# SSD layer of a four-layer network: B and C projected once with taps on VectorE, mask added to the decay sums, y summed in PSUM

## The chip, the cores and the metric

The kernel runs on one core of a Trainium2 chip. The core has five engines, each with its own queue of instructions in a fixed order: TensorE (PE in the profile, with its weight loads as PEld), VectorE (DVE), ScalarE (ACT), GpSimd (POOL) and SyncE (SP), which here only issues transfers. An instruction that waits holds up everything behind it in its engine's queue. The metric is the device time of one execution in microseconds (us); the time of a kernel is the median of its runs.

## The reference, cut to what matters

The program is four layers on an image batch of 4 x 96 x 64 x 64: a Mamba block, an SSD layer (Mamba 2, scanned in four directions), a second Mamba block, and a ConvNeXt block. Only the SSD layer is changed. Per direction it computes, for a sequence of 4096 tokens with 96 channels:

```python
zxbcdt = xs @ in_proj_w.T
z = zxbcdt[..., :D_INNER]                                  # 192
xBC = zxbcdt[..., D_INNER:D_INNER + CONV_DIM]              # x 192, B 128, C 128
dt = softplus(zxbcdt[..., D_INNER + CONV_DIM:] + dt_bias)  # 3 heads
xBC = silu(conv_b + sum(conv_w[:, i] * xp[:, i:i + l, :] for i in range(4)))
...
dAc = cumsum(dt * A)                                       # within a chunk
diff = dAc[:, :, :, None, :] - dAc[:, :, None, :, :]
seg = exp(where(mask, diff, -inf))
att = einsum('bcsn,bctn->bcst', Cm, Bm)[..., None] * seg * dt
y = einsum('bcsth,bcthp->bcshp', att, xh)                  # within a chunk
y = y + einsum(..., Cm, exp(dAc), prev)                    # from the carried state
y = rmsnorm((y + D * xh) * silu(z)) @ out_proj_w.T
```

xp is xBC padded by three tokens, so the depthwise convolution has four taps. Results do not depend on the chunk length; the kernel uses 128.

## The kernel before, in words

The whole program is one stream of instructions. The class `Ssd` handles the layer. Four images, two orders (row by row, column by column) and two directions (r = 0 forward, r = 1 reverse) give 16 sequences; each sequence is four blocks of 1024 tokens, and each block eight chunks of 128. That makes 64 blocks and 512 chunks. The normalised input of one order stands in SBUF in `xn`, 96 channels by 4096 tokens, with three zero columns at each end and one row of ones below.

`weights_of` prepares weights once. It multiplies the projection weights of x, B and C by each of the four convolution taps, so that projection and convolution become one product with an inner size of 4 x 96 = 384, which `sconv` holds in three pieces of 128 rows. `stack` fills `pk`, the matching right-hand side: four shifted copies of the input, packed into three pieces of 128 rows by six transfers on SP's queue.

`front` does, for a block, everything that does not depend on the scan. For r = 0 it projects z (L1051) and copies it out. Then for B and C (q = 0, 1) and each half of 512 tokens it accumulates three products of `sconv` with `pk` in a PSUM bank (L1069), which ScalarE copies out with the bias (L1074). Then for each chunk it forms x, token by channel, in three products (L1080) and DVE adds the bias (L1085). Then one Silu over x, B and C (L115, between two loads of function tables), for r = 0 one over z, and B is transposed (L1097, copied by L1099). All of these use two PSUM banks with the tag "front".

Per chunk four stages follow. `decay` takes the cumulative sums of the chunk's tokens, broadcast to all partitions by a transfer (`dr`), subtracts the partition's own sum and clamps at zero (L1118, one DVE instruction per head), and takes one Exp over three heads (L110). `weights` forms C times B in PSUM (L1131), multiplies it with the triangular mask on DVE (L1133), multiplies the decays by that on POOL (L1134), and has POOL form x times dt, x times the state weights and x times D in one instruction (L1138). `outputs` multiplies decays with x for three heads (L1163), multiplies C with the carried state (L1168), scales that on DVE (L1172), adds D times x on POOL (L1173), adds the product within the chunk on DVE (L1174), updates the carried state (L1177 on PE, L1182 on POOL, L1183 on DVE), multiplies with z (L1185), and squares on ScalarE (L1186). `scale`, `by_channels` (L1204, L1206) and `finish` (L1217, L1228) normalise, transpose, project and add into the output, a pair of chunks at a time.

`run` interleaves: per chunk it calls `weights` one chunk ahead, `outputs` for the chunk, `finish` three behind, `decay` two ahead, and after each of these four points takes one step of `front` for the next block; steps end at the `yield`s. `preludes` (normalisation, turning, step sizes of the next sequence) advance likewise. This is only the order in which the program is written; a scheduler then sets the order on each engine, and inserts the waits. Tiles of a tag are reused in turn, so an instruction that writes a tile waits for the readers of the one `bufs` before it: two "front" banks, two "y" banks, four `seg`, three `xs`.

Of the kernel before, what the change touches and what calls it, by code (L numbers as in the profile page):

```python
# [18 lines left out]
F32 = mybir.dt.float32  # L19
# [8 lines left out]
P = 128  # L28
T = 512
# [741 lines left out]
)  # L771


class Ssd:


# [5 lines left out]
    def __init__(self, ctx, tc, k, src, dst, w):  # L782
        nc = self.nc = tc.nc
        self.k, self.w, self.dst = k, w, dst
        self.raw, self.res, self.bn, self.src = src
        one = self.one = ctx.enter_context(tc.tile_pool(name="s1", bufs=1))
        self.work = ctx.enter_context(tc.tile_pool(name="swork", bufs=2))
        self.psum = ctx.enter_context(tc.tile_pool(name="sps", bufs=2, space=PSUM))
        self.dram = ctx.enter_context(tc.tile_pool(name="sdram", bufs=2, space=DRAM))

        self.norm = one.tile([C, 1], F32, name="norm")
        nc.sync.dma_start(self.norm, w["norm"])
        self.ones = one.tile([P, P], F32, name="ones")
        nc.vector.memset(self.ones, 1.0)
        self.eps = one.tile([C, 1], F32, name="epsn")
        nc.vector.memset(self.eps, 1.1920929e-07)

        self.tri = one.tile([P, 2, Q], F32, name="tri")
        for r, step in enumerate((1, -1)):
            nc.gpsimd.affine_select(  # L800
                out=self.tri[:, r], in_=self.ones, compare_op=ALU.is_ge, fill=0.0, base=0,
                pattern=[[step, Q]], channel_multiplier=-step,
            )


        self.xn = [one.tile([C + 1, L + 2 * PAD], F32, name=f"xn{o}") for o in range(2)]
        for x in self.xn:
            nc.vector.memset(x[:C, :PAD], 0.0)
            nc.vector.memset(x[:C, PAD + L :], 0.0)
            nc.gpsimd.memset(x[C : C + 1], 1.0)  # L810
        self.prev = self.pk = None
        self.X = one.tile([C, L], F32, name="X")
        self.batch = None
        self.seq = {}
        self.z = {}

    def weights_of(self, w):
# [3 lines left out]
        nc.sync.dma_start(self.inw, w["in"])  # L821

        conv = self.work.tile([P, 3 * BLK], F32, tag="pk", name="conv")
        conv = conv[:C, : 4 * CONV].rearrange("c (k n) -> c k n", k=4)
        nc.sync.dma_start(conv, w["conv_wT"].partition_broadcast(C))
        yield
        xbc = self.inw[:C, DI : DI + CONV]
        nc.vector.tensor_tensor(conv, conv, xbc[:, None].to_broadcast([C, 4, CONV]), ALU.mult)
        self.conv = one.tile([P, 3, CONV], F32, name="sconv")
        for i, r0, r1, tap, c0 in PIECES:  # L830
            nc.sync.dma_start(self.conv[r0:r1, i], conv[c0 : c0 + r1 - r0, tap])
        self.xbias = one.tile([P, DI], F32, name="xbias")
# [2 lines left out]
        nc.sync.dma_start(  # L835
            self.bcbias, w["in"][C, 2 * DI : 2 * DI + 2 * DST].rearrange("(q p) -> p q", q=2)
        )
        self.ad = one.tile([P, 2, NH], F32, name="ad")
        nc.sync.dma_start(self.ad, w["ad"].partition_broadcast(P))
        self.a = one.tile([P, 1, NH], F32, name="a")  # L840
# [138 lines left out]
    def decays(self, r):  # L979
# [12 lines left out]
        ps = self.bank("front")  # L992
        nc.tensor.matmul(ps[:, :n], lhsT=self.tri[:, r], rhs=da, start=True, stop=True)
        nc.vector.tensor_copy(dac, ps[:, :n])
        nc.tensor.matmul(ps[:, n : 2 * n], lhsT=self.ones, rhs=da, start=True, stop=True)
        k.act.exp_ln(dec, ps[:, n : 2 * n], AF.Exp)
        k.act.exp_ln(edac, dac, AF.Exp)
# [10 lines left out]
        nc.vector.tensor_copy(row, pt)  # L1008
        rows = self.dram.tile([n, Q], F32, name="rows")
        nc.sync.dma_start(rows, row)  # L1010
        return dict(dac=dac, dec=dec, edac=edac, coef=coef, rows=rows)

    def prelude(self, b, o, r):

# [20 lines left out]
    def front(self, b, o, r, blk, made, following):  # L1035
# [26 lines left out]
        pre = self.work.tile([P, n1 + n2], F32, name="pre")  # L1062
        x = made["x"] = pre[:, :n1].rearrange("p (c n) -> p c n", c=QB)
        bc = made["bc"] = pre[:, n1:].rearrange("p (q t) -> p q t", q=2)
        for q in range(2):
            for c in range(BLK // T):
                p = self.bank("front")
                for i in range(3):
                    nc.tensor.matmul(  # L1069
                        p, lhsT=self.conv[:, i, DI + q * DST : DI + (q + 1) * DST],  # L1070
                        rhs=pk[:, i, ds(c * T, T)], start=(i == 0), stop=(i == 2),
                    )
                    yield
                nc.scalar.activation(  # L1074
                    bc[:, q, ds(c * T, T)], p, AF.Identity, bias=self.bcbias[:, q : q + 1]
                )
        for c in range(QB):
            p = self.bank("front")[:, :DI]
            for i in range(3):
# [31 lines left out]
    def decay(self, g):  # L1111

        nc, k = self.nc, self.k
        blk, c, made = g["blk"], g["c"], g["made"]
        n0 = (blk * QB + c) * NH
        seg = g["seg"] = self.work.tile([P, NH, Q], F32, name="seg", bufs=4)
        for h in range(NH):
            nc.vector.tensor_scalar(  # L1118
                seg[:, h], g["pair"]["dr"][:, c % 2 * NH + h],
                made["dac"][:, n0 + h : n0 + h + 1], 0.0, ALU.subtract, ALU.min,  # L1120
            )
        k.act.exp_ln(seg, seg, AF.Exp)

    def weights(self, g):

        nc = self.nc
        c, made, seg = g["c"], g["made"], g["seg"]
        bm, cm = (made["bc"][:, q, ds(c * Q, Q)] for q in range(2))
        self.halves = self.bank("halves").rearrange("p (i n) -> p i n", i=2)
        ps = self.halves[:, 0, :Q]  # L1130
        nc.tensor.matmul(ps, lhsT=bm, rhs=cm, start=True, stop=True)  # L1131
        cb = self.work.tile([P, 1, Q], F32, name="cb")
        nc.vector.tensor_tensor(cb[:, 0], self.tri[:, g["r"]], ps, ALU.mult)  # L1133
        nc.gpsimd.tensor_tensor(seg, seg, cb.to_broadcast([P, NH, Q]), ALU.mult)  # L1134
        xs = self.work.tile([P, 3, NH, HD], F32, name="xs", bufs=3)
        x = made["x"][:, c].rearrange("p (k h d) -> p k h d", k=1, h=NH)
        coef = made["coef"][:, g["blk"] * QB + c, :, :, None]
        nc.gpsimd.tensor_tensor(  # L1138
            xs, x.to_broadcast([P, 3, NH, HD]), coef.to_broadcast([P, 3, NH, HD]), ALU.mult
        )  # L1140
        g["xs"] = xs.rearrange("p k h d -> p k (h d)")

    def outputs(self, g):
# [19 lines left out]
            nc.tensor.matmul(py[:, ch], lhsT=seg[:, h], rhs=xs[:, 0, ch], start=True, stop=True)  # L1163
        y = self.work.tile([P, DI], F32, name="y")
        if first:
            nc.vector.tensor_tensor(y, py[:, :DI], xs[:, 2], ALU.add)
        else:
            nc.tensor.matmul(  # L1168
                py[:, DI : 2 * DI], lhsT=made["bc"][:, 1, ds(c * Q, Q)], rhs=self.prev,
                start=True, stop=True,  # L1170
            )
            nc.vector.tensor_tensor(heads(y), heads(py[:, DI : 2 * DI]), by_head("edac"), ALU.mult)  # L1172
            nc.gpsimd.tensor_tensor(y, y, xs[:, 2], ALU.add)  # L1173
            nc.vector.tensor_tensor(y, y, py[:, :DI], ALU.add)  # L1174
        if not last:
            st = self.halves[:, 1, :DI]
            nc.tensor.matmul(st, lhsT=made["bt"][:, c], rhs=xs[:, 1], start=True, stop=True)  # L1177
# [4 lines left out]
                nc.gpsimd.tensor_tensor(heads(prev), heads(self.prev), by_head("dec"), ALU.mult)  # L1182
                nc.vector.tensor_tensor(prev, prev, st, ALU.add)  # L1183
            self.prev = prev
        nc.vector.tensor_tensor(yz[:, i], y, made["z"][:, c], ALU.mult)  # L1185
        nc.scalar.activation(y, yz[:, i], AF.Square, accum_out=ssq[:, i : i + 1])  # L1186

    def scale(self, g):
# [482 lines left out]
```

## Time and profile before

| | |
|---|---|
| median of 3 runs | 9310.08 us (9306.05 to 9322.33) |
| profiled execution, its own time | 9324.82 us |
| its span, first to last instruction | 9323.1 us |
| mean granted clock of TensorE | 0.925 |
| PE busy | 7912.3 us |
| DVE busy | 7734.4 us |
| POOL busy | 6984.1 us |
| ACT busy | 5461.1 us |
| SSD stage, from its first B/C matmul to about its end | 2864.7 to 5880 us of the span |

The profile comes from one execution. Busy time is the time in which an engine has an instruction running; matmuls overlap, and their ends are modelled, so a sum of matmul durations can exceed the time they took. In a row of groups stand the line, the engine, the operation, output and inputs, shapes and count, then busy time in us and the mean duration of one in ns, then the idle time of the engine just before, and what ended it. A row of a timeline has the start, the time, the engine, the line and the operation.

### The profile page before, as it was taken

The numbers are of one execution on the slowest core, as the hardware profiler recorded it, in microseconds if no ns is written. First come the engines' busy times: TensorE is split into PE (matmuls) and PEld (weight loads), VectorE is DVE, ScalarE is ACT, GpSimd is POOL, SyncE is SP. The second block draws the span as 40 slices with busy tenths as digits, with TensorE's granted clock in tenths as the row PEclk, the third lists the DMA queues.
The fourth block names the chain that finished last, engine by engine and source line by source line (L and its number), as shares of the span: only waits on it lengthen the run. The fifth ranks groups of instructions, "written<-read, shape, count | busy, mean of one in ns | idle before, by whom it ended". The sixth has DMA issues, their size and how long they took to land. (4 is left out here: it accounts for less than half of the span.)

```text
span 9323.1 us, 114005 instructions
## 1 busy us (share of the span) xinstructions
PE 7912.3 (85%) x34968; PEld 3427.8 (37%) x34968; DVE 7734.4 (83%) x9136; ACT 5461.1 (59%) x9510; POOL 6984.1 (75%) x4637
## 2 busy tenths in 40 slices
PE   7888888888878988998898989788888888888588
PEld 1222222222215676676776767412222222222122
DVE  6999999999995676666666667699999999999787
ACT  5667666666654454555545544566766666666255
POOL 6999999999994555555555555599999999999411
PEclk8999999999988998999999999899999999998789
DMA  7888888888873223222322222488888988888643
GB/s 184 217 228 229 220 225 230 221 227 221 224 197 100 68 76 87 69 69 82 86 62 79 82 69 70 113 211 225 230 218 225 234 220 221 231 222 223 153 115 83
DMA packets 799372, 1525.85 MB, mean 164 GB/s; under 512 B 114510, under 2 KB 120042, under 8 KB 795691
## 3 DMA queue, kind: packets, MB, share of 16 engines
q1 hardware_dynamic: 795690, 1513.45, 62.6%
q8 instruction: 280, 4.59, 0.2%
q10 hardware_dynamic: 3072, 5.11, 0.2%
q14 instruction: 330, 2.70, 0.1%
HBM read 1222.94 MB, written 148.50 MB: 147 GB/s over the span
## 5 line engine op out<-in xcount | busy, mean ns | idle before, releaser
L419 POOL TENSOR_TENSOR hc<-hs,bc 128x1024 f32<-128x1024 f32 x1536 | 3606.0, 2364 | 298.1 <-DVE hs L412 287.7
L412 DVE TENSOR_TENSOR_SCAN hs<-da,carry,bs 128x1024 f32<-128x1024 f32 x864 | 2027.4, 2347 | 129.7 <-issue 51.2
L384 PE MATMUL bs<-du,seldu 64*128 64x512 f32 x4608 | 1480.4, 709 | 687.8 <-DVE hs L412 672.0
L407 DVE TENSOR_TENSOR bs<-bs,bc 128x1024 f32<-128x1024 f32 x1152 | 1397.3, 1213 | 19.4 <-PE bs L384 18.5
L110 ACT ACTIVATE da<-da,w_a 128x1024 f32<-128x1024 f32 x1152 | 1301.6, 1138 | 1.5
L384 PEld LDWEIGHTS bs<-du,seldu 64*128 64x128 f32 x4608 | 408.8, 202 | 1766.6 <-issue 887.1
L433 PE MATMUL py<-hc,selsum 128*32 128x512 f32 x6144 | 868.1, 627 | 94.4 <-DVE y L450 70.7
L392 POOL TENSOR_TENSOR du<-du,bc 128x1024 f32<-128x1024 f32 x384 | 909.0, 2367 | 12.6 <-DMA du<-dg 12.6
L1118 DVE TENSOR_SCALAR seg<-dr,dac 128x128 f32<-128x128 f32 x1536 | 639.0, 449 | 296.1 <-PE y L1163 292.5
L1134 POOL TENSOR_TENSOR seg<-seg,cb 128x384 f32<-128x384 f32 x512 | 515.9, 1009 | 475.4 <-DVE cb L1133 409.4
L207 PE MATMUL pu<-h,w_conv 96*64 96x512 f32 (+1 forms) x3072 | 809.4, 646 | 7.8 <-ACT h L196 7.2
L1069 PE MATMUL front<-pk,sconv 128*128 128x512 f32 x1536 | 760.6, 612 | 24.5 <-ACT z L1057 21.0
L110 ACT ACTIVATE bs<-da,w_a 128x1024 f32<-128x1024 f32 x384 | 428.4, 1116 | 585.3 <-DVE hs L412 472.6
L1173 POOL TENSOR_TENSOR y<-y,xs 128x192 f32<-128x192 f32 x496 | 294.6, 594 | 611.7 <-DVE y L1172 594.6
L412 DVE TENSOR_TENSOR_SCAN hs<-bs,carry,du 128x1024 f32<-128x1024 f32 x288 | 670.8, 2329 | 58.9 <-DMA dd<-delta 30.8
L1186 ACT ACTIVATE y<-yz 128x192 f32<-128x192 f32 x512 | 186.1, 363 | 906.7 <-DVE yz L1185 905.7
L412 DVE TENSOR_TENSOR_SCAN hs<-da,bs 128x1024 f32<-128x1024 f32 x288 | 658.6, 2287 | 42.5 <-issue 14.6
L1138 POOL TENSOR_TENSOR xs<-pre,coef 128x576 f32<-128x576 f32 x512 | 598.8, 1174 | 58.1 <-ACT pre L115 25.5
L1080 PE MATMUL front<-sconv,pk 128*128 128x192 f32 x3072 | 572.7, 330 | 54.4 <-DVE pre L1085 49.1
L1080 PEld LDWEIGHTS front<-sconv,pk 128*128 128x128 f32 x3072 | 497.2, 190 | 86.6 <-DVE pre L1085 75.7
L1163 PEld LDWEIGHTS y<-xs,seg 128*128 128x128 f32 x3072 | 440.4, 205 | 144.4 <-issue 83.9
L1163 PE MATMUL y<-xs,seg 128*128 128x64 f32 x3072 | 445.1, 281 | 27.8 <-POOL seg L1134 22.3
(228 smaller groups left out, 13854.6 us busy)
## 6 DMA issues: line engine op xcount, KB each, us to landing
da<-dd SPq DMA_DIRECT2D x3072, 256.0 KB
du<-dg SPq DMA_DIRECT2D x768, 256.0 KB
dr<-rows SPq DMA_DIRECT2D x256, 384.0 KB
bc<-rows SPq DMA_DIRECT2D x256, 256.0 KB
dd<-delta SPq DMA_DIRECT2D x192, 256.0 KB
dg<-du SPq DMA_DIRECT2D x192, 256.0 KB
pk<-xn SPq DMA_DIRECT2D x128, 384.0 KB
pk<-xn SPq DMA_DIRECT2D x128, 256.0 KB
```

The source lines that it names most:

```text
L110: self.last = self.scalar.activation(out, in_, func, **kw)
L207: nc.tensor.matmul(pu[HALFP * i : HALFP * (i + 1)], lhsT=wt["conv"][:kk, tap, D0[j] : D0[j] + HALFP], rhs=h[:kk, ds(i * T + tap, T)], star ...
L384: nc.tensor.matmul(g["bs"][:, i], lhsT=self.sel["du"][rows, g["half"], g["q"]], rhs=g["made"]["du"][rows, g["j"]], start=True, stop=True,)
L392: self.tc.nc.gpsimd.tensor_tensor(g["du"], g["du"], self.b_or_c(g, 0), ALU.mult)
L407: nc.vector.tensor_tensor(dbx, dbx, self.b_or_c(g, 0), ALU.mult)
L412: nc.vector.tensor_tensor_scan(out, da, dbx, init, ALU.mult, ALU.add)
L419: nc.gpsimd.tensor_tensor(g["hc"], hs, self.b_or_c(g, 1), ALU.mult)
L433: nc.tensor.matmul(py[ds(HALFP * i + QUART * x["half"], QUART)], lhsT=self.sel["sum"][:, q], rhs=x["hc"][:, i], start=(q == 0), stop=(q == ...
L1069: nc.tensor.matmul(p, lhsT=self.conv[:, i, DI + q * DST : DI + (q + 1) * DST], rhs=pk[:, i, ds(c * T, T)], start=(i == 0), stop=(i == 2),)
L1080: nc.tensor.matmul(p, lhsT=pk[:, i, ds(c * Q, Q)], rhs=self.conv[:, i, :DI], start=(i == 0), stop=(i == 2),)
L1118: nc.vector.tensor_scalar(seg[:, h], g["pair"]["dr"][:, c % 2 * NH + h], made["dac"][:, n0 + h : n0 + h + 1], 0.0, ALU.subtract, ALU.min,)
L1163: nc.tensor.matmul(py[:, ch], lhsT=seg[:, h], rhs=xs[:, 0, ch], start=True, stop=True)
```

## The change

B and C are no longer convolved by the product. `project` multiplies the plain projection weights with 345 (or 343) columns of `xn`, three more than the 342 (or 340) tokens of a stretch, in one product per stretch; `STRETCHES` cuts the 1024 tokens into three. ScalarE copies the bank out, multiplied by the last tap and with the bias; `convolve` then adds the other three taps, each a multiply-add on DVE that reads the same bank at a shifted column and updates the output in place. `convolve` runs one stretch behind `project`, and so both banks are held in between. The steps (`yield`) of the part are twelve, as before. `sconv` and its preparation shrink to x, and two small loads bring the taps.

In `decay`, POOL adds a mask (0 or -1e30) to the broadcast sums of three heads in one instruction, and ScalarE takes one Exp per head with the negated own sum as its bias (`ndac`). In `weights`, DVE multiplies the decays with the product in PSUM directly; the DVE product with the mask and POOL's product are gone. In `outputs`, y is summed in its PSUM bank, and the product with z reads it from there.

```diff
+STRETCHES = ((0, 342), (342, 342), (684, 340))
@@ __init__
+        self.mask = one.tile([P, 2, 1, Q], F32, name="mask")
+        nc.vector.tensor_scalar(
+            self.mask[:, :, 0], self.tri, 1.0, 1e30, ALU.subtract, ALU.mult
+        )
@@ weights_of
-        conv = conv[:C, : 4 * CONV].rearrange("c (k n) -> c k n", k=4)
-        nc.sync.dma_start(conv, w["conv_wT"].partition_broadcast(C))
+        conv = conv[:C, : 4 * DI].rearrange("c (k n) -> c k n", k=4)
+        nc.sync.dma_start(conv, w["conv_wT"][:, :DI].partition_broadcast(C))
         yield
-        xbc = self.inw[:C, DI : DI + CONV]
-        nc.vector.tensor_tensor(conv, conv, xbc[:, None].to_broadcast([C, 4, CONV]), ALU.mult)
-        self.conv = one.tile([P, 3, CONV], F32, name="sconv")
+        xs = self.inw[:C, DI : 2 * DI]
+        nc.vector.tensor_tensor(conv, conv, xs[:, None].to_broadcast([C, 4, DI]), ALU.mult)
+        self.conv = one.tile([P, 3, DI], F32, name="sconv")
...
+        self.taps = one.tile([P, 2, 4], F32, name="taps")
+        for q in range(2):
+            of = w["conv_wT"][:, DI + q * DST : DI + (q + 1) * DST]
+            nc.sync.dma_start(self.taps[:, q], of.rearrange("k p -> p k"))
@@ decays
+        ndac = self.work.tile([P, n], F32, name="ndac")
+        nc.vector.tensor_scalar_mul(ndac, dac, -1.0)
@@ front
+        begun = []
+
+        def project(q, t0, n):
+            p = self.bank("front")
+            nc.tensor.matmul(
+                p[:, : n + 3], lhsT=self.inw[:C, 2 * DI + q * DST : 2 * DI + (q + 1) * DST],
+                rhs=xn[:C, ds(base + t0 + (0 if r == 0 else PAD), n + 3)], start=True, stop=True,
+            )
+            out = bc[:, q, ds(t0, n)]
+            shifts = [p[:, ds(tap if r == 0 else 3 - tap, n)] for tap in range(4)]
+            nc.scalar.activation(
+                out, shifts[3], AF.Identity, bias=self.bcbias[:, q : q + 1],
+                scale=self.taps[:, q, 3:4],
+            )
+            begun.append((q, out, shifts))
+
+        def convolve():
+            q, out, shifts = begun.pop(0)
+            for tap in range(3):
+                nc.vector.scalar_tensor_tensor(
+                    out, shifts[tap], self.taps[:, q, tap : tap + 1], out, ALU.mult, ALU.add
+                )
+
         for q in range(2):
-            for c in range(BLK // T):
-                p = self.bank("front")
-                for i in range(3):
-                    nc.tensor.matmul(
-                        p, lhsT=self.conv[:, i, DI + q * DST : DI + (q + 1) * DST],
-                        rhs=pk[:, i, ds(c * T, T)], start=(i == 0), stop=(i == 2),
-                    )
+            for t0, n in STRETCHES:
+                project(q, t0, n)
+                yield
+                if len(begun) == 2:
+                    convolve()
                     yield
-                nc.scalar.activation(
-                    bc[:, q, ds(c * T, T)], p, AF.Identity, bias=self.bcbias[:, q : q + 1]
-                )
+        convolve()
+        yield
@@ decay
+        nc.gpsimd.tensor_tensor(
+            seg, g["pair"]["dr"][:, ds(c % 2 * NH, NH)],
+            self.mask[:, g["r"]].to_broadcast([P, NH, Q]), ALU.add,
+        )
         for h in range(NH):
-            nc.vector.tensor_scalar(
-                seg[:, h], g["pair"]["dr"][:, c % 2 * NH + h],
-                made["dac"][:, n0 + h : n0 + h + 1], 0.0, ALU.subtract, ALU.min,
-            )
-        k.act.exp_ln(seg, seg, AF.Exp)
+            k.act.exp_ln(seg[:, h], seg[:, h], AF.Exp, bias=made["ndac"][:, n0 + h : n0 + h + 1])
@@ weights
-        cb = self.work.tile([P, 1, Q], F32, name="cb")
-        nc.vector.tensor_tensor(cb[:, 0], self.tri[:, g["r"]], ps, ALU.mult)
-        nc.gpsimd.tensor_tensor(seg, seg, cb.to_broadcast([P, NH, Q]), ALU.mult)
+        nc.vector.tensor_tensor(seg, seg, ps[:, None].to_broadcast([P, NH, Q]), ALU.mult)
@@ outputs
-            nc.vector.tensor_tensor(y, py[:, :DI], xs[:, 2], ALU.add)
+            nc.vector.tensor_tensor(py[:, :DI], py[:, :DI], xs[:, 2], ALU.add)
...
-            nc.vector.tensor_tensor(y, y, py[:, :DI], ALU.add)
+            nc.vector.tensor_tensor(py[:, :DI], y, py[:, :DI], ALU.add)
...
-        nc.vector.tensor_tensor(yz[:, i], y, made["z"][:, c], ALU.mult)
+        nc.vector.tensor_tensor(yz[:, i], py[:, :DI], made["z"][:, c], ALU.mult)
```

More of the change, by code (lines that the diff above doesn't have):

```diff
@@ L1010, in decays @@
         nc.sync.dma_start(rows, row)
-        return dict(dac=dac, dec=dec, edac=edac, coef=coef, rows=rows)
+        return dict(ndac=ndac, dec=dec, edac=edac, coef=coef, rows=rows)
     def prelude(self, b, o, r):
```

## The prediction

> **What bounds the kernel now.** I read the page first (busy shares, then the 40 slices), then the stretch of time in which the changed code runs, cut into the parts of one block, then the costliest groups on each engine there, and last the timeline of single instructions. The chain that ended last says nothing here: its steps sum to some 6% of the span, at the end, in another stage.
>
> ```profile
> PE 7912.3 (85%) x34968; PEld 3427.8 (37%) x34968; DVE 7734.4 (83%) x9136; ACT 5461.1 (59%) x9510; POOL 6984.1 (75%) x4637
> ...
> PE   7888888888878988998898989788888888888588
> PEld 1222222222215676676776767412222222222122
> DVE  6999999999995676666666667699999999999787
> ...
> POOL 6999999999994555555555555599999999999411
> ```
>
> PEld marks the stage: slices 13 to 25, where weight loads are dense, are the SSD layer. There PE is the fullest engine and DVE and POOL have room. Everywhere else DVE and POOL are at 9, and the change touches nothing there.
>
> ```profile
> 2864.70:5880.00 3015.30, 2707.98 (x14596) 2104.46 (x14594) 2050.36 (x5203) 1523.69 (x3472) 1656.68 (x2008) 0.95 0.26 75
> ...
> 4446.20:4463.00 16.80, 16.75 (x76) 10.91 (x77) 11.99 (x30) 8.38 (x23) 10.00 (x13) 1.00 0.70 202
> 4463.00:4475.10 12.10, 11.47 (x77) 11.16 (x76) 8.41 (x24) 1.81 (x6) 5.09 (x7) 1.00 0.42 107
> 4475.10:4491.40 16.30, 12.40 (x87) 10.80 (x85) 11.60 (x31) 13.79 (x27) 11.87 (x14) 1.00 0.43 125
> ```
>
> Busy times by stretch, in the order PE, weight loads, DVE, ACT, POOL. The first row is the whole SSD stage, 3015 us for 64 blocks, 47.1 us each. The other three are one forward block, cut at its first B/C matmul (L1069), its first x matmul (L1080) and the end of its last: a "BC" stretch of 16.8 us, an "x" stretch of 12.1 and a rest of 16.3, in sum 45.2. In BC, PE has no gap at all; in the rest PE idles, and ACT (13.8 of 16.3, the big Silu and its table loads) is the fullest. A reverse block, cut likewise at 4575.6, is 17.8, 13.5 and 9.1, in sum 40.4. So the stage has two bounds in turn.
>
> ```profile
> L1118 DVE TENSOR_SCALAR seg<-dr,dac 128x128 f32<-128x128 f32 x1519 | 629.0, 447 | 294.9 <-PE y L1163 291.2 <-DMA dr<-rows 3.5
> L1185 DVE TENSOR_TENSOR yz<-y,z 128x192 f32<-128x192 f32 x503 | 421.4, 838 | 9.1
> L1085 DVE TENSOR_TENSOR pre<-front,xbias 128x192 f32<-128x192 f32 x512 | 175.3, 351 | 188.3 <-PE front L1080 188.0
> ...
> L1133 DVE TENSOR_TENSOR cb<-tri,halves 128x128 f32<-128x128 f32 x504 | 140.1, 282 | 190.8 <-PE halves L1131 110.5 <-POOL seg L1134 79.4
> ...
> L1134 POOL TENSOR_TENSOR seg<-seg,cb 128x384 f32<-128x384 f32 x503 | 506.9, 1009 | 472.2 <-DVE cb L1133 408.4 <-ACT seg L110 39.9 <-ACT dtrow L961 8.5
> ...
> 4404.41 1.16 POOL L1138 TENSOR_TENSOR xs<-pre,coef 128x576 f32<-128x576 f32 x1
> ...
> 4404.75 1.02 DVE L1185 TENSOR_TENSOR yz<-y,z 128x192 f32<-128x192 f32 x1
> ```
>
> Groups of the stage, then two timeline rows. L1185 and L1085 have the same size, but L1185, which reads two SBUF tensors, takes 838 ns and L1085, which reads PSUM, 351. The timeline shows why: yz starts while POOL's xs runs and ends 0.2 us after it.
>
> **What the Trainium skill says.** "SBUF — State Buffer", section "SBUF: two separate sides": a DVE instruction with two SBUF inputs and a GpSimd one that reads SBUF lock each other out for a whole instruction. The L1185 rows agree. "VectorE: DVE Perf Modes", "The TRN2 errata": an fp32 tensor_tensor takes (N+151)/0.96 ns; L1085 (192: 357, trace 351) agrees, L1185 does not, being locked. "Perfetto Trace Analysis", "Identifying the Most-Contended Engine": matmul busy time is no good measure of the PE's limit. So I take spacings for PE: weight loads of L1069 begin 0.43 us apart in the timeline, though one matmul is 612 ns on the page.
>
> **The change, part by part, summed over the stage.** PE: each product is two recorded matmuls. Gone are 1536 x 0.43 = 660 us; new are 64 blocks x 6 products x 2 x 0.43 x 345/512 = 223. PE: -437. ACT: three Exp of 128 columns for one of 384. The rows L110 at 1024 (1138 ns) and 384 (518) give 0.97 ns a column, so 128 is 270, +0.29 x 512 = +150 in durations (about 100 in spacing, ACT instructions overlap by 0.1 us in the timeline). L1074 becomes 384 of (675 - 165) = 0.51 instead of 256 of 0.675: +23. POOL: the product by cb becomes the mask's addition in the same shape: 0; bounds from L1182 (192 columns, 574) to L1138 (576, 1174), I take 1009. DVE: L1118 goes, -1536 x 0.447 = -687; cb, -512 x 0.282 = -144; yz, now from PSUM, 0.838 to 0.35, -250. New: the product seg by PSUM, 384 columns, 351 + 192 x 0.984 = 0.54 (slope from L266, 512 columns, 666 ns), +276; 1152 tap instructions of 342 columns from PSUM, 0.50 each, +576. That slope is of a three-operand instruction from PSUM, but none of this size is shown; bounds 0.36 (342 columns at 0.96 a ns and 0.04 of start) and 0.57 (L1463, two SBUF operands, 846 at 512 columns, scaled); I take 0.50. DVE: -229. The in-place sum in PSUM costs what L1174 costs now. At the start two small tap loads go onto SP's queue ahead of the first pk loads (0.41 us each by the bcbias row, and pk is wanted later now); the weight product L828 shrinks from 2.02 to about 0.9 us; ndac is 16 x 0.2 = 3 us. All these run under the normalisation of the first batch, about 30 us; without that cover they'd be 2 to 5 us.
>
> **What of this is on the path.** No engine is full after it, so I follow the order of instructions in the changed program for the same two blocks. The BC work is moved from PE, where it stood back to back, to DVE, and the scheduler now puts 4 chunks of eight into that stretch instead of 2.5.
>
> BC, forward: DVE issues 18 taps x 0.50 = 9.0, four chunks x (4 x 0.35 + 0.54) = 7.8, two copies yt and two additions to X 1.9: 18.7, less 0.04 for each of 40 overlaps (starts are that much closer than durations) 17.1. PE needs only 12 x 0.29 = 3.5 and, for four chunks, 4 x 2.15 = 8.6 (starts in the timeline from 4402.03: y, carried state and new state 1.32 a chunk; L1131 0.22; transposes and output projection 1.2 a pair). What is late next: POOL's mask additions are queued two at a time ahead of y+D*x (L1203), and the second waits for its seg buffer, that is for y matmuls of the next chunk. DVE's sum of y stands behind it, about 1.2 us once a block. Together 18.3, against 16.8.
>
> x: 24 products at 0.325 (12 recorded matmuls start within 1.95) = 7.8, one chunk's matmuls 1.3, a wait for DVE 0.7: 9.8, against 12.1, because fewer chunks are left there.
>
> Rest: ACT from the last x: table 1.28, Silu 3.19, z 1.47, table 1.28, then copies, six or seven Exp at 0.17 spacing, two scalings, 7.6: 14.9, against 16.3. Sum 43.0 against 45.2, -2.2. The reverse block the same way: 21.0, 10.1, 7.3: 38.4 against 40.4, -2.0.
>
> Three blocks of eight carry the next sequence's normalisation or step sizes and are paced by that too; I count half there: 40 x 2.1 + 24 x 1.05 = -109 us, +3 for ndac. Against the profiled span, 9323 - 106 = 9217. That execution took 9324.8, the median is 9310.1, so 9202; I say 9200.
>
> **Rivals.**
> PE is the bound throughout. For: 90% busy, no gap in BC. Against: PE idles in the rest, ACT is full there. Then most of 437 is kept: 8870 to 9050.
>
> Nothing changes: taps on DVE cost each BC stretch what x and rest give. With taps at 0.57 instead of 0.50 a block loses 18 x 0.07 = 1.3 us of the 1.7 that it gains on average. For: DVE sums to 17 us in an 18 us stretch. Against: L266's slope. Time 9285 to 9330.
>
> Slower, by POOL's queue: mask additions now stand ahead of L1203 and wait for matmuls of a later chunk, which wait for DVE, which waits for L1203's result. I have priced one such wait of 1.2. If three of the four rounds of a BC stretch each lose a mask addition and a y addition (1.0 + 0.59), that is 4.8 - 1.2 = 3.6 more than priced, 1.9 net a block, 64 x 1.9 = +122, about 9430. It decides from 1.7 us a block on. For: POOL's L1173 already waits 592 us for DVE in this stage. Against: these waits cost nothing today.
>
> **How the numbers follow.** My case, 9120 to 9290: 0.46. PE's relief mostly kept, under 9120: 0.19. No change: 0.12. Slower, 9330 to 9450: 0.23 (the POOL mechanism at half its price to its full). A measurement of this kernel tells about 0.2% from no change. The likeliest case's own range is 9120 to 9290; leaving out about a tenth at each end of all cases gives 9010 to 9380. Faster 0.65, same 0.12, slower 0.23.
>
> **What would show it.** Right: tap instructions near 0.50 us; yz at 0.35; PE idle in BC, with DVE over 90% busy there; the BC stretch a little longer, x and rest shorter; ACT idle before Silu. Wrong: DVE waiting more than about 1.7 us a block on POOL for y; taps above 0.57; or PE still without a gap in BC, which would mean the bigger gain.

## The result, and the profile after

The changed kernel takes 9185.08 us (median of 4 runs, 9178.76 to 9191.85) against 9308.06 us (median of 4 runs of the kernel before, 9302.81 to 9322.33): a ratio of 0.9866 [0.9849, 0.9883], 123 us less. The prediction was 9200 us. Its own sum was made against the profiled execution of before (9324.82 us); the profiled execution of the changed kernel took 9178.76, 146 less where the sum had 106 less. That pair flatters the change, as the profiled run of before is slower than all four of its timed runs and that of the changed kernel the fastest of its four.

The page of the changed kernel: busy time, share and count of each engine, then two rows of the 40 slices.

```profile
PE 7611.2 (83%) x34200; PEld 3366.9 (37%) x34200; DVE 7597.2 (83%) x8769; ACT 5724.8 (62%) x10662; POOL 6929.5 (76%) x4637
...
PE   7888888888877888888888888788888888888588
DVE  6999999999995666666666667699999999999787
```

PE lost 301 us of busy time, not the 437 of the prediction, which counted spacings; DVE lost 137, ACT gained 264. In the SSD stage (slices 13 to 25) PE no longer reaches 9. From the first to the last block's first B/C matmul the stage went from 2975.0 to 2829.9 us in the timelines, 145 of the 146 us, so everything outside it kept its length.

Busy times by stretch of the changed kernel (columns: PE, weight loads, DVE, ACT, POOL, granted clock, DMA share, GB/s). First most of the stage, then a forward and a reverse block, each as BC, x and rest. The reverse block is the one that the prediction cut, number 37 of the 64. The forward one is number 35, the one after the block that it cut (number 34).

```profile
2867.00:5740.00 2873.00, 2436.42 (x13831) 2052.45 (x13830) 1920.81 (x4852) 1786.21 (x4616) 1605.20 (x2012) 0.91 0.27 79
...
4423.90:4441.50 17.60, 14.33 (x85) 10.92 (x84) 14.26 (x36) 11.97 (x38) 10.95 (x15) 1.00 0.15 46
4441.50:4451.50 10.00, 9.92 (x62) 9.62 (x63) 6.82 (x20) 1.89 (x5) 4.23 (x6) 1.00 0.12 39
4451.50:4468.50 17.00, 13.94 (x82) 12.88 (x81) 7.49 (x20) 13.88 (x31) 9.87 (x12) 0.80 0.42 117
4503.60:4524.40 20.80, 15.88 (x93) 12.21 (x93) 15.62 (x39) 14.88 (x47) 12.24 (x17) 1.00 0.17 55
4524.40:4534.80 10.40, 10.08 (x61) 9.42 (x62) 7.26 (x21) 3.49 (x9) 5.29 (x7) 1.00 0.01 2
4534.80:4540.80 6.00, 5.40 (x44) 4.87 (x42) 3.83 (x11) 5.45 (x6) 4.69 (x6) 1.00 0.64 185
```

PE, which had no gap in BC before, now idles there (14.33 of 17.60). The stretches against the prediction, in us:

| | BC | x | rest | sum |
|---|---|---|---|---|
| forward block, before | 16.8 | 12.1 | 16.3 | 45.2 |
| predicted | 18.3 | 9.8 | 14.9 | 43.0 |
| measured, the block after it | 17.6 | 10.0 | 17.0 | 44.6 |
| that block, before | 16.8 | 12.1 | 17.8 | 46.6 |
| reverse block, before | 17.8 | 13.5 | 9.1 | 40.4 |
| predicted | 21.0 | 10.1 | 7.3 | 38.4 |
| measured | 20.8 | 10.4 | 6.0 | 37.2 |
| mean of all 64 blocks, before | 18.2 | 12.6 | 16.5 | 47.2 |
| mean of all 64 blocks, after | 20.4 | 10.5 | 14.0 | 44.9 |

Block 34 itself took 19.8, 10.0 and 16.1 us in the changed kernel, at a granted clock of 0.74 in its BC, where it had 1.00 before. So I compare block 35 with itself: its rest had a clock of 0.81 before and of 0.80 after. The means of the rest are over 63 blocks, as none follows the last.

The groups of the changed kernel in the stage: on DVE the taps, the product by C times B, and yz; on POOL the mask's addition; on ACT the Exp of one head and the copy with the last tap.

```profile
L1096 DVE SCALAR_TENSOR_TENSOR pre<-front,taps,pre 128x342 f32<-128x342 f32 (+1 forms) x1152 | 619.3, 563 | 49.1 <-ACT pre L1087 38.2 <-DMA gn<-in_L_gnorm 10.5
L1164 DVE TENSOR_TENSOR seg<-seg,halves 128x384 f32<-128x384 f32 x504 | 274.0, 544 | 49.2 <-ACT seg L110 44.4 <-PE halves L1163 4.2
L1215 DVE TENSOR_TENSOR yz<-y,z 128x192 f32<-128x192 f32 x503 | 176.0, 350 | 4.6
L1149 POOL TENSOR_TENSOR seg<-dr,mask 128x384 f32<-128x384 f32 x507 | 507.6, 1001 | 532.8 <-PE y L1193 436.5 <-DVE pre L1096 29.0 <-ACT pre L1087 13.8
L110 ACT ACTIVATE seg<-seg,ndac 128x128 f32<-128x128 f32 x1514 | 516.7, 391 | 51.1 <-POOL seg L1149 50.6
L1087 ACT ACTIVATE pre<-front,bcbias,taps 128x342 f32<-128x342 f32 (+1 forms) x384 | 240.8, 630 | 195.9 <-PE front L1081 192.6 <-DMA rows<-row 1.3
```

Three of the six prices are as predicted: L1164 544 ns (540), yz 350 (350), the mask's addition 1001 (1009). A tap takes 563 where 500 was taken, just within its bound of 570. The two on ACT are off: 391 where 270 was taken, 630 where 510 was.

### The profile page after: what moved, and what is told of

The parts are those of the page before. It is cut to its first block, busy times and chain, and to the rows that moved or that the text cites. A ratio compares the mean times of both kernels' runs of the same rounds, so it can differ in the third digit from the quotient of the medians.

```text
span 9177.0 us, 113399 instructions
## 1 busy us (share of the span) xinstructions
PE 7611.2 (83%) x34200; PEld 3366.9 (37%) x34200; DVE 7597.2 (83%) x8769; ACT 5724.8 (62%) x10662; POOL 6929.5 (76%) x4637
## 5 line engine op out<-in xcount | busy, mean ns | idle before, releaser
L1149 POOL TENSOR_TENSOR seg<-dr,mask 128x384 f32<-128x384 f32 x512 | 512.6, 1001 | 532.8 <-PE y L1193 436.5
L1096 DVE SCALAR_TENSOR_TENSOR pre<-front,taps,pre 128x342 f32<-128x342 f32 (+1 forms) x1152 | 619.3, 563 | 49.1 <-ACT pre L1087 38.2
L110 ACT ACTIVATE seg<-seg,ndac 128x128 f32<-128x128 f32 x1536 | 524.4, 391 | 55.8 <-POOL seg L1149 55.1
L1112 PEld LDWEIGHTS front<-sconv,pk 128*128 128x128 f32 x3072 | 525.0, 198 | 65.3 <-DVE pre L1117 19.2
L1203 POOL TENSOR_TENSOR y<-y,xs 128x192 f32<-128x192 f32 x496 | 294.6, 594 | 290.5 <-DVE y L1202 284.1
L1493 DVE SCALAR_TENSOR_TENSOR acc<-strips,kern,acc 128x512 f32<-128x512 f32 x504 | 424.1, 843 | 53.2 <-ACT acc L1483 36.7
```

The lines of the kernel that those rows point to most:

```text
L110: self.last = self.scalar.activation(out, in_, func, **kw)
L1096: nc.vector.scalar_tensor_tensor(out, shifts[tap], self.taps[:, q, tap : tap + 1], out, ALU.mult, ALU.add)
L1112: nc.tensor.matmul(p, lhsT=pk[:, i, ds(c * Q, Q)], rhs=self.conv[:, i, :DI], start=(i == 0), stop=(i == 2),)
L1493: nc.vector.scalar_tensor_tensor(acc, stacks[i][1][:, y : y + strip, x : x + WW], kern[:, g, tap : tap + 1], acc, ALU.mult, ALU.add,)
```

## The experiments

The change has three parts that can be made alone: B and C by taps ("bc"), the mask addition ("mask"), and y in PSUM ("y"). The first five runs, with the kernels before and after and a seventh, make all eight combinations. Medians are in us; ratios are to the runs of the kernel before that belong to each (their medians lie between 9308.06 and 9314.74), with 95% intervals. "Less" is always against those, and two experiments are compared by what each is less. The intervals are some 15 to 25 us to each side for most of them, so a difference of under 30 us between two is not clear of the noise; where I lean on one, I say what the timelines add.

**y in PSUM alone.** Three operands of the kernel before; the third, in the first chunk of a sequence, goes likewise:

```diff
-            nc.vector.tensor_tensor(y, y, py[:, :DI], ALU.add)
+            nc.vector.tensor_tensor(py[:, :DI], y, py[:, :DI], ALU.add)
-        nc.vector.tensor_tensor(yz[:, i], y, made["z"][:, c], ALU.mult)
+        nc.vector.tensor_tensor(yz[:, i], py[:, :DI], made["z"][:, c], ALU.mult)
```

> The kernel before, with only y summed in its PSUM bank. Theory (two bounds in turn: PE in the BC stretch, ScalarE after the Silu): yz falls from 838 to about 350 ns, DVE loses some 250 us of busy time, and the time hardly moves, 0 to 40 us faster than before, since PE has no gap in BC. Rival (the lock between DVE and POOL holds up the stage): at least 100 us faster. Also: POOL's xs and prev get shorter if they too waited for the lock.

Measured: 9162.65, ratio 0.9842 [0.9821, 0.9863], 146 us less. This part alone gains at least as much as the whole change. The theory of the expectation, by which the product with z was hidden, falls. The groups before, on DVE and POOL (2864 to 5680 us):

```profile
L1185 DVE TENSOR_TENSOR yz<-y,z 128x192 f32<-128x192 f32 x465 | 391.0, 841 | 8.3
...
L1182 POOL TENSOR_TENSOR prev<-prev,dec 128x192 f32<-128x192 f32 x437 | 250.7, 574 | 192.0 <-PE y L1168 161.9 <-DVE seg L1118 13.0 <-DVE prev L1183 11.4
```

and with y in PSUM:

```profile
L1185 DVE TENSOR_TENSOR yz<-y,z 128x192 f32<-128x192 f32 x496 | 174.8, 352 | 9.0
...
L1182 POOL TENSOR_TENSOR prev<-prev,dec 128x192 f32<-128x192 f32 x466 | 239.3, 513 | 122.0 <-PE y L1168 83.7 <-DVE seg L1118 24.4 <-DVE prev L1183 10.7
```

The same instruction takes 352 ns instead of 841, and POOL's update of the state, unchanged in the program, 513 instead of 574. Both sides of a lock became shorter, as the Trainium skill has it ("SBUF — State Buffer", "SBUF: two separate sides": a two-SBUF-input DVE instruction and a GpSimd one that reads SBUF keep each other out).

**The mask addition alone**, from `decay` and `weights` of the change; two small tiles ("da" and "wt") have one buffer instead of two, to make room, here and in the next experiment:

```diff
-            nc.vector.tensor_scalar(seg[:, h], dr[...], dac[...], 0.0, ALU.subtract, ALU.min)
-        k.act.exp_ln(seg, seg, AF.Exp)
+        nc.gpsimd.tensor_tensor(seg, dr[...], self.mask[...], ALU.add)
+        for h in range(NH):
+            k.act.exp_ln(seg[:, h], seg[:, h], AF.Exp, bias=made["ndac"][...])
-        nc.gpsimd.tensor_tensor(seg, seg, cb.to_broadcast([P, NH, Q]), ALU.mult)
+        nc.vector.tensor_tensor(seg, seg, ps[:, None].to_broadcast([P, NH, Q]), ALU.mult)
```

> The kernel before, with only the mask addition on POOL, one Exp per head and the product with PSUM on DVE. Theory: DVE loses some 550 us, ScalarE gains about 340 (Exp of 128 columns 391 ns in the changed kernel), PE keeps its work, so the BC stretch stays PE-bound at 16 to 18 us and the time is within 40 us of before. Rival (DVE is what limits): 100 us faster or more. The rival of POOL's queue: slower than before by over 50 us.

Measured: 9233.81, ratio 0.9915 [0.9897, 0.9932], 75 us less. On average a forward block grew from 44.6 to 46.1 us, all of it in the rest (17.0 to 18.6), where ACT is the fullest engine and now has three Exp for one; a reverse block shrank from 49.9 to 45.4, in its rest too (16.0 to 11.6).

**Both of these**, B and C left on PE:

> The changed kernel without the B and C part. Theory: DVE is down to about 1400 us in the stage and still the time is within 60 us of before, as PE stays without a gap in BC. Rival (these two parts make the whole gain): about 9185.

Measured: 9166.74, ratio 0.9839 [0.982, 0.9857], 142 us less: no faster than y alone. The rows of the stage of this kernel, and then of y alone, in the columns as above:

```profile
2864.00:5720.00 2856.00, 2648.42 (x14532) 2097.85 (x14532) 1432.31 (x3681) 1728.98 (x4470) 1601.38 (x2002) 0.95 0.28 79
```

```profile
2864.00:5740.00 2876.00, 2642.33 (x14711) 2076.40 (x14709) 1841.60 (x5254) 1526.16 (x3508) 1641.18 (x2034) 0.97 0.28 79
```

DVE has 409 us less to do than with y alone, and the time stays; PE is at 93%. This doesn't show that room on DVE is worth nothing with y in PSUM, for the part also gives ACT 203 us more and puts POOL's instruction ahead of the Exp, and it has two effects that cancel: against y alone, forward blocks are 2.1 us longer and reverse ones 1.7 shorter. The same holds in all five pairs of kernels here that differ in the mask addition (in the first two pairs in the two small tiles too): with it the mean forward block is longer, by 1.4 to 2.7 us, and the mean reverse block shorter, by 0.7 to 4.4. The addition in the reverse direction alone was not run.

**B and C by taps alone**, the `front` and `weights_of` parts of the change:

> The kernel before, with only the B and C part. Theory: PE loses its 437 us, but DVE keeps L1118 and the locked yz and gets 1152 taps of 0.56 us, so DVE with some 2600 us of 2900 becomes the bound of the stage: 0 to 200 us slower than before. Rival (PE's relief is the whole gain and DVE has room): 9185 or less.

Measured: 9296.46, ratio 0.9985 [0.9978, 0.9992], 12 us less. The row of its stage:

```profile
2864.00:5720.00 2856.00, 2370.72 (x13231) 1961.25 (x13231) 2280.44 (x6069) 1529.63 (x3460) 1570.61 (x1917) 0.92 0.28 77
```

PE is relieved (83% of the stretch) and DVE is at 80%, with yz, 621 ns here, still a slow one among its work. The mean block has a BC stretch longer by 1.7 us, an x and a rest shorter by 0.9 and 1.3.

**Taps and y, no mask addition:**

> The kernel before with the B and C part and y in PSUM, without the mask addition. The gain of y in PSUM alone was 146 us, of the B and C part alone 12. Theory A (the locked yz was what held the stage, and once it is gone PE's work counts again): the relief of PE now pays, under 9120. Theory B (the BC stretch passes from PE to DVE and gives nothing either way): 9150 to 9180. Theory C (DVE is full with taps and L1118): over 9200.

Measured: 9185.28, ratio 0.986 [0.9845, 0.9875], 129 us less; without its mask addition the changed kernel takes neither more nor less time (6 us between them).

**The changed kernel with y in SBUF as before:**

```diff
-            nc.vector.tensor_tensor(py[:, :DI], y, py[:, :DI], ALU.add)
+            nc.vector.tensor_tensor(y, y, py[:, :DI], ALU.add)
-        nc.vector.tensor_tensor(yz[:, i], py[:, :DI], made["z"][:, c], ALU.mult)
+        nc.vector.tensor_tensor(yz[:, i], y, made["z"][:, c], ALU.mult)
```

> The changed kernel with y summed in SBUF again, so that yz reads two SBUF tensors. If the lock costs what it cost before wherever DVE is the pacing engine: yz back to about 0.8 us, 64 x 8 x 0.45 = 230 us of DVE, and 70 to 200 us slower than the changed kernel (9255 to 9385), that is about level with the kernel before. If the mask addition or the taps carry the gain: under 9230.

Measured: 9273.41, ratio 0.9962 [0.9952, 0.9972], 36 us less; 87 of the 123 are gone with these operands. Its product with z:

```profile
L1215 DVE TENSOR_TENSOR yz<-y,z 128x192 f32<-128x192 f32 x472 | 323.6, 686 | 4.6
```

Here, too, the time follows yz: 686 ns instead of 350. The eight combinations, us against the kernel before:

| | without y | with y |
|---|---|---|
| neither | 0 | -146 |
| mask | -75 | -142 |
| bc | -12 | -129 |
| bc and mask | -36 | -123 |

Reading across, y is worth 67 to 146 us in every row. Reading down the right column, the mask addition adds nothing to it (+4, +6), and moving B and C costs 17 to 19 us (+17, +19), which is about what these runs can tell apart. In the left column that move costs 39 on top of the mask and brings 12 by itself.

The timelines show where the 17 to 19 stand. Eight blocks make the two directions of one image and order, and in the eighth the step sizes and decays of the next sequence are prepared, which need the two "front" banks as well. On top of y, with the mask addition or without it, the move makes an eighth block 8.5 to 8.7 us longer, some 60 us over the seven that have a sequence after them, and saves 0.7 to 1.0 us in each of the 56 others, 40 to 56 us. So in seven blocks of eight the whole move pays, a little; that the banks are the reason in the eighth is read from the timelines and was not tested.

**The changed kernel without its taps.** The three multiply-adds are left out, so B and C are not convolved:

```diff
-            q, out, shifts = begun.pop(0)
-            for tap in range(3):
-                nc.vector.scalar_tensor_tensor(...)
+            begun.pop(0)
```

> The changed kernel with the three tap instructions on DVE left out, so that B and C are not convolved. It prices the taps on the path: 1152 of them at 0.49 us spacing are 564 us of DVE. If the BC stretch is DVE-bound, it falls from 20.4 us to PE's or ScalarE's time, about 13 to 15: 64 x 6 = 380 us faster than the changed kernel, about 8800. If something else paces the stretch (POOL's queue, ScalarE), it is under 150 us faster.

Measured: 8840.49, ratio 0.9492 [0.9476, 0.9508], 474 us less, 351 below the changed kernel. The mean BC stretch falls from 20.4 to 13.2 us, though PE has the same matmuls: the taps set its length in the changed kernel, by DVE's time or by the banks that they keep; this run takes both away.

**Half of it: B as three products on PE, C by taps, y in PSUM, no mask addition.** If the whole move overfills DVE and no move leaves PE full, a part of it should beat both. `sconv` keeps B's columns besides x's.

```diff
+        for c in range(BLK // T):
+            ...            # B, bc[:, 0]: three products on PE, as before
+        for t0, n in STRETCHES:
+            project(1, t0, n)    # C: one product and taps, as in the change
+            ...
```

> As the run before it, but only C is projected with taps; B stays three products on PE. PE loses some 218 us of work, DVE gets 576 taps, about 280 us in spacing. Theory A and B: between y alone (9163) and both; if PE and DVE share the BC stretch evenly, faster than either, 9080 to 9150. Theory C: 9160 to 9200.

Measured: 9067.34, ratio 0.9735 [0.972, 0.975]. That is 247 us less than before, and 124 below the changed kernel: it beats both, and y alone by 101. The row of most of its stage:

```profile
2870.00:5350.00 2480.00, 2221.78 (x12779) 1810.94 (x12778) 1829.62 (x5194) 1385.88 (x3202) 1454.18 (x1807) 0.96 0.29 84
```

PE is at 90% and DVE at 74%. BC takes 18.1 us, x 10.3, the rest 14.6: the shorter x and most of the shorter rest of the change, without the longer BC. Against y alone an eighth block is 3.8 us longer, not 8.7, and the others are 2.2 shorter, not 0.7. So the half gains in both places: there is less on DVE, and the banks are held for less of the stretch. No run parts the two.

**The same half with the mask addition**, that is, the changed kernel with B on PE:

> The changed kernel with B left to three products on PE and only C projected with taps; mask addition and y in PSUM as in the change. If the BC stretch of the changed kernel is paced by DVE (18 taps, of which 9 go) and PE has room for 12 more matmuls of 0.43 us, it shortens by some 2 us a block: 9050 to 9100. If the mask addition's ScalarE load after the Silu binds, it is no better than half the taps with y alone (9067), up to 9110.

Measured: 9126.31, ratio 0.9802 [0.9777, 0.9826]; 183 us less, 60 below the changed kernel and 64 above the half without the mask addition. Here the mask addition costs: forward blocks are 2.7 us longer and reverse ones only 0.7 shorter.

**Why it costs: the Exp of one head?** The changed kernel with one Exp over three heads, the own cumulative sum left out of the decays:

```diff
-        for h in range(NH):
-            k.act.exp_ln(seg[:, h], seg[:, h], AF.Exp, bias=made["ndac"][...])
+        k.act.exp_ln(seg, seg, AF.Exp)
```

> The changed kernel with one Exp over three heads, without the bias, so that the token's own cumulative sum is left out of the decays. It prices the split Exp: 3 x 391 ns against about 520. If ScalarE paces the forward blocks' rest (13.9 busy of 17.0 us), 32 blocks save 1 to 2 us each: 9100 to 9150. If ScalarE is hidden: 9170 or more.

Measured: 9142.11, ratio 0.9823 [0.9799, 0.9848], 167 us less, 44 below the changed kernel. Its Exp:

```profile
L110 ACT ACTIVATE seg<-seg 128x384 f32<-128x384 f32 x512 | 263.1, 518 | 224.2 <-POOL seg L1149 222.3
```

One of 518 ns for three of 391: 254 us less on ACT, of which 44 are on the path. The rest falls by 0.7 us on average in the forward blocks, to 15.7, and by 0.8 in the reverse ones, and BC grows by 0.4 in both. Against the 64 above, the Exp can be the larger part of what the mask addition costs there; the run was not made on that kernel, so this is argued.

**POOL's queue: five `seg` buffers for four.**

```diff
-        seg = g["seg"] = self.work.tile([P, NH, Q], F32, name="seg", bufs=4)
+        seg = g["seg"] = self.work.tile([P, NH, Q], F32, name="seg", bufs=5)
```

> The changed kernel with five seg buffers in place of four, so that POOL's mask addition waits for the y matmul of a chunk further back (436 us of POOL waiting in the changed kernel), and D times x behind it is not held. If that wait is what DVE's sum of y pays for (263 us of waiting, against 63 before): 50 to 150 us faster, 9035 to 9135. If the scheduler only moves the additions further ahead: within 30 us of 9185.

Measured: 9189.21, ratio 0.9872 [0.9848, 0.9896]: no change. The chain that it was to remove is in the timeline of the changed kernel, in the BC stretch at the place that the prediction named (in brackets the idle time before and its releaser):

```profile
4430.04 0.34 DVE L1202 TENSOR_TENSOR y<-y,edac 128x192 f32<-128x192 f32 x1
...
4430.78 0.99 POOL L1149 TENSOR_TENSOR seg<-dr,mask 128x384 f32<-128x384 f32 x1 [1.18 <-PE y L1193]
4431.73 0.59 POOL L1203 TENSOR_TENSOR y<-y,xs 128x192 f32<-128x192 f32 x1
4432.35 0.36 DVE L1204 TENSOR_TENSOR y<-y 128x192 f32<-128x192 f32 x1 [1.49 <-POOL y L1203]
```

DVE's product by `edac` is done at 4430.38, but L1203 starts only at 4431.73, behind a mask addition that waited for matmuls. The waits of the changed kernel over the stage (us in total, times, longest):

```profile
POOL seg L1149 <- PE y L1193: 436.5, 197, 5.2
...
DVE y L1204 <- POOL y L1203: 263.4, 373, 3.3
```

and with five buffers:

```profile
POOL seg L1149 <- PE y L1193: 465.7, 208, 5.2
...
DVE y L1204 <- POOL y L1203: 262.8, 360, 3.2
```

The fifth buffer didn't take the wait away: the scheduler moves the additions with it. So this run doesn't price the wait.

**Does y's gain come from DVE's time alone?** With y in PSUM alone, a copy of about yz's saving was put behind yz on DVE, from PSUM, 320 columns (the two small tiles have one buffer here too):

```diff
         nc.vector.tensor_tensor(yz[:, i], py[:, :DI], made["z"][:, c], ALU.mult)
+        spare = self.work.tile([P, 2, 160], mybir.dt.bfloat16, name="spare", bufs=1)
+        nc.vector.tensor_copy(spare, py[:, None, :160].to_broadcast([P, 2, 160]))
```

> y in PSUM alone, with a copy of 320 columns from PSUM added on DVE right behind yz, about 0.49 us, which gives back the busy time that yz lost without the lock (two small once-per-sequence tiles are single-buffered for room). If yz's time on DVE's queue was what counted: back to 9280 or more. If the lock did harm beyond DVE's time (POOL held up as well) or the scheduler's order did: stays under 9200.

Measured: 9236.43, ratio 0.9916 [0.9901, 0.9931]. The copy:

```profile
L1188 DVE CAST spare<-y 128x320 bf16<-128x320 f32 x503 | 241.1, 479 | 0.0
```

It occupies DVE for 479 ns, close to the 489 that yz lost, and gives back 68 of the 146 us. The copy also reads y's bank, which comes free later, so up to about half of the gain goes with DVE's occupied time. The rest may be POOL's, no longer held up, or the order: in the stage 80% of DVE's instructions stand at the place that they have in the kernel before, against 95% with y alone. That stays open.

## Why the prediction was right, and where it was not

**The number.** 9200 against 9185; predicted -106 us, measured -123 between medians. The sign, the size and the shape of a block came out: BC longer, x and rest shorter, the mean block -2.3 us for the -2.1 that the two cut blocks gave. That the total came so close is luck in part: the sum put the gain in the wrong place, as the experiments show, and its errors cancelled. Two slips in it are small: 342 columns at 0.96 a ns and 0.04 more are 0.40 us, not the 0.36 given as a tap's lower bound, and -106 from the median is 9204, as the 9202 mixes the profile's span with the time.

**BC.** Right in length, 17.6 and 20.8 for 18.3 and 21.0, and right in kind: PE idles, and without the taps the stretch is a third shorter. The inner terms were off and cancelled. I counted 42 DVE instructions in the forward BC, 17.1 us, and 1.2 us of waiting; there are 36, 14.26 us, as three chunks stand in the stretch and not four, and so 3.3 us of waiting. One wait is the predicted one on POOL, 1.49 us (the last row shown with the five buffers). Another, 1.28, is for the copy with the last tap (L1087): ACT's copy, three taps and the freeing of a bank follow each other, and that chain I did not price. DVE is at 81% there, not over 90.

**The tap.** 563 ns for 500, yet the sum held, because DVE's instructions start closer together than they last. From the timeline of the changed kernel (start, time, count at the end):

```profile
4434.58 2.01 DVE L1096 SCALAR_TENSOR_TENSOR pre<-front,taps,pre 128x340 f32<-128x340 f32 x4
...
4438.90 2.96 DVE L1096 SCALAR_TENSOR_TENSOR pre<-front,taps,pre 128x342 f32<-128x342 f32 x6
```

Six in 2.96 us with the last 0.56 long start 0.48 apart. The Trainium skill's price for an fp32 tensor_tensor ("VectorE: DVE Perf Modes", "The TRN2 errata") gives an estimate of (342 + 151)/0.96 = 514 ns for this size. The tap is another instruction, a scalar_tensor_tensor with one factor per partition, and takes 563; it starts 480 to 490 ns before the next, and the measurement decides.

**x.** Right: 10.0 and 10.4 for 9.8 and 10.1.

**Rest.** Wrong in both directions. Forward, it shrank by 0.6 us on average (17.0 to 16.4) and by 0.8 in the block measured (17.8 to 17.0), where the prediction had 1.4. Two things pull against each other. With B and C by taps, ACT loads the table before the last x is done: the Silu starts 0.4 us after the end of the last x product, where it was 1.9 before (means of the forward blocks). That gains 1.4 us, which the prediction didn't have: its sum starts with the table load. From the end of the second table load to the next BC it then takes 10.1 us on average instead of 9.3, and there the term that failed is ACT's: "three Exp of 128 columns for one of 384" at 270 ns each. They take 391, and stand 0.29 us apart in the timeline (four in 1.27 us) where I took 0.17; with one Exp it is 9.4 us again. In the block measured ACT also waits 2.96 us for the products of z (L1063): from 4458.9 us on, the clock granted to PE was half for 6.8 us.

The reverse rest was shorter than predicted (6.0 for 7.3), and the prediction shows no term for the reason. In the timeline of the kernel before, in that block:

```profile
4612.83 2.32 DVE L1118 TENSOR_SCALAR seg<-dr,dac 128x128 f32<-128x128 f32 x3
...
4615.40 0.80 PE L1131 MATMUL halves<-pre 128*128 128x128 f32 x2 [2.62 <-DVE cb L1133]
...
4615.99 1.91 PE L1069 MATMUL front<-pk,sconv 128*128 128x512 f32 x2
```

The next BC (L1069) stood on PE behind a product of C and B (L1131), which waited for the DVE product with the triangle (L1133), and that one stood on DVE behind three subtractions (L1118) that took 2.32 us. In the changed kernel both DVE instructions are gone, and the next BC waits for a "front" bank only:

```profile
4540.19 0.57 ACT L1131 COPY bt<-front 128x512 f32<-128x512 f32 x1
...
4540.81 0.85 PE L1081 MATMUL front<-xn,inw 96*128 96x345 f32 x2 [0.31 <-ACT bt L1131]
```

This comes with the mask addition: in the five pairs that differ in it, the mean reverse rest is 2.5 to 4.4 us shorter with it, and the mean forward rest 0.8 to 2.1 longer.

**The blocks with a prelude.** "I count half there" was not so. By the position of a block in a group of eight, the five plain blocks save 1.4 us each, not 2.1, and the three others together 10.4, not 3.2: two of them save 8.1 and 7.5, one, the eighth, loses 5.1. In that one both "front" banks are held between `project` and `convolve` while the decays of the next sequence need them (its BC went from 21.2 to 28.6 us on average); the reading is from the timelines, no run was made for it.

**The step that failed: where the gain is.** The prediction had it in PE's relief ("the stage has two bounds in turn"), with yz as 250 us in DVE's balance, needed to make room for the taps. Its size was right (838 to 350 ns) and its place was not. Taken alone, the change of yz's operand is worth 146 us, PE's relief alone 12, and on top of y the relief costs 17 to 19. "In BC, PE has no gap at all" was true of BC, but x and rest, where DVE, POOL and PE wait for each other once a chunk, had a locked instruction of 0.84 us in each round. With y the mean x and rest are shorter by 0.8 and 1.3 us, BC by 0.4. How much of that is DVE's own time and how much POOL's or the order is what the copy behind yz left open.

**The rivals.** PE as the bound throughout: no, for the taps took its place (351 us without them). But it has its truth in the half: where only C is moved, PE's relief brings another 101 us over y alone. No change: the taps' duration reached 563 of its 570, but their spacing did not. Slower by POOL's queue: the waits are there, 263 us, 4.1 a block against 1.0 before (62.5 us on L1174), well past the 1.7 at which it was to decide, and the kernel is faster. The mark was wrong: it took every wait of DVE to be on the path. How much of the waiting stood beside other work is open, as the fifth buffer did not remove it.

## What to carry to other kernels

Look for instructions of one size with two durations before looking for work to move: here 841 against 351 ns at 192 columns said that one SBUF operand, put into the PSUM bank that was there anyway, was worth more than the rest of the change. When work is moved from one full engine to another, try a part of it as well: on top of y, both B and C on DVE cost 17 us, C alone gained 101. Look at the kinds of blocks apart before calling a part worthless: the mask addition, 4 to 6 us with y in total, lengthens forward blocks and shortens reverse ones, and what the whole move loses stands in one block of eight. And run the parts singly: the right total (-106 for -123) came from a wrong account of its parts.

## What the hardware showed that I had not expected

A per-partition operand on ACT has a price that the slope over sizes doesn't show: Exp of 128 columns with a bias from SBUF takes 391 ns, where 384 columns without one take 518 and the slope gave 270. Two instructions of two columns in the changed kernel, 256 of each, show it best: the Ln with a bias (`eps`) takes 286 ns in the median, the Exp without one 199.

The granted clock of TensorE was lower in every kernel that projects both B and C in one pass and runs their taps. In the stretch from 2870 to 5350 us it is 0.89 to 0.92 in six such kernels, and 0.94 to 0.97 in the seven others, the half among them, as also in the one that has the products without the taps (0.95). So the products of 345 columns are not the cause by themselves. The row of the changed kernel, to be read beside that of the half:

```profile
2870.00:5350.00 2480.00, 2105.15 (x11877) 1766.62 (x11877) 1651.17 (x4169) 1541.16 (x3969) 1379.44 (x1727) 0.91 0.28 81
```

PE is also idler in the six: it is busy for 83 to 86% of the stretch there, and for 88 to 93% in the eight others. The clock records of two traces say more. In the changed kernel the clock is halved 62 times in this stretch, for 3.4 us or a few times that; in the 3.4 us before, PE was busy for 45% of the time on average (75% at most); where the clock stayed full, PE was busy for 89% in the 3.4 us before, on average. In the half it is halved 29 times, after 48% against 92%. So in these traces the lower clock follows idle stretches of PE, and the changed kernel has more of them; no run varied that alone. One matmul of x takes 341 ns there against 330 before, so the lower clock is in the durations too, and part of what PE's relief failed to bring may be in it.
